# A four-layer graph network on one core: reordered ends, a tanh in two steps, and rows summed by accumulating DMA

## The chip, the core and the metric

The kernel runs on one core of a Trainium2 chip. The metric is the device time of one execution in microseconds. The engines named below are PE (TensorE: matmuls, with PEld for its weight loads), DVE (VectorE), ACT (ScalarE), POOL (GpSimd) and SP (SyncE, which here only issues DMA transfers).

## The reference, cut to what matters

64 graphs of 256 nodes with 128 features, all in fp32, go through four layers; every layer is a layernorm with ReLU ahead of it and a residual behind it. Layer 0 is the costly one: it needs a score for every pair of nodes, with a leaky ReLU over 256 features inside.

```python
# layer 0, W = adj
s1 = einsum('bkf,ef->bke', x, W[:, :F]);  s2 = einsum('bkf,ef->bke', x, W[:, F:])
pre = s1[:, :, None, :] + s2[:, None, :, :] + b_lin      # 256 x 256 pairs x 256 features
h = where(pre >= 0, pre, 0.2 * pre)
e = einsum('bije,e->bij', h, a) + bias
out = sigmoid(softmax(e, axis=2) @ x)
# layer 1
e = sigmoid(a_tgt + a_src + be) * mask;  recv = elu([e @ x_h, x_h * sum(e)] @ Wn + bn)
# layer 2: attention with A = exp(8 * tanh(q k / (8 sqrt(d)))) * adj
# layer 3: five steps of a gated update
for _ in range(5):
    m = adj @ h
    z = sigmoid([m, m] @ w3.T + h @ u3.T + b);  r = sigmoid([m, m] @ w4.T + h @ u3.T + b)
    hv = tanh([m, m] @ w5.T + (r * h) @ u5.T + b);  h = (1 - z) * h + z * hv
```

## The kernel before

**Groups.** The 64 graphs are cut into 34 groups (line 15): two of one graph, thirty of two, two of one. Layers 1 to 3 work on a group at a time; layer 0's pairs are made for one graph at a time.

**The pairs of layer 0** (class `Pairs`, from line 538). A graph has 32 rows of 8 receiving nodes each. For a row and each half `ec` of the 256 features there is a batch: one SBUF tile `r` of 128 partitions x 4 x 2 x 256 numbers, 8 KB in each partition and 1 MB in all, which holds max(s2, -s1) or relu(s2 + s1). A batch is made in two halves, and each half by whichever of three engines is free: DVE with one instruction (line 614), ACT with four (line 626), POOL with four (line 631). `r` has 11 buffers (`BUFS`). PE then reads a finished batch with eight matmul instructions (line 679) and adds it into the scores `e_ps`. So a row costs PE two batches. There is one way to save PE a batch: a *merged* row has only the batch of the first feature half made, and DVE adds the second half into it in place with eight instructions of line 648; then PE reads one batch. A row is merged when at least `SPARE` = 5 finished batches wait for PE as it begins.

**A planner writes the order of every engine's instructions.** The loop at the end of the function keeps a modelled time for PE, DVE, ACT and POOL (class `Model`) and, again and again, issues the step that can start first: a half, a merge, a batch for PE, or the next step of one of the chains. The chains are generators that give the name of the engine for the next step: `ahead` (layernorm and sender tiles of the next graphs), `behind` (layer 0's softmax), `chain12` (layers 1 and 2), `chain3` (layer 3, one group after another, and the constants at the start) and `chain4` (layer 3 of the last group alone). In the middle they are paced, so that chain work is spread. The order is fixed once it is written: on the chip each engine goes through its own list in order and waits for semaphores where the model was wrong.

**The start.** ACT issues the DMAs of the adjacency matrix, of layer 0's `a`, and of ten small vectors (all through line 139), and runs its first activation after them. `constants0` (line 216) sorts the features by the sign of `a` and makes `w_p` (the sorted, scaled weights, from four pairs of matmuls and one ACT copy, line 283), `blin_p`, `v2_rep` and what is needed for an odd feature. `head` (line 463) makes the first group's s1 and s1n, `senders` (line 512) its s2; pair making starts when s2 is there.

**The end.** After the last pair, the last group still goes through its softmax, layers 1, 2 and 3. `Home` (line 899) gives the last group's layer 3 banks and tiles of its own, so that it can run beside `chain3`. In a step of `layer3` (line 916) ACT runs the tanh of z and then the one of the candidate.

Of the kernel before, what the change touches and what calls it, by code (L numbers as in the profile page):

```python
# [8 lines left out]
F32 = mybir.dt.float32  # L9
AF = mybir.ActivationFunctionType  # L10
ALU = mybir.AluOpType
# [9 lines left out]
SPARE = 5  # L21
MARGIN = {"pe": 300}
MEMORY = 7000
# [13 lines left out]
class Model:  # L37
# [8 lines left out]
    def __init__(self):  # L46
        self.t = {"pe": 0.0, "dve": 0.0, "act": 0.0, "pool": 0.0}
# [6 lines left out]
def kernel(ctx: ExitStack, tc: tile.TileContext, ins: dict, out: bass.AP):  # L54
# [87 lines left out]
    def column(name):  # L142

        v = ins[name]
        return fetch(
            [P, v.shape[0] // P], "c_" + name, v.rearrange("(c p) -> p c", p=P), nc.scalar
        )

    order = ctx.enter_context(tc.manual_schedule())
    xts = [load_x(0)]  # L150
    adj_n = fetch([P, 2, N], "adj_n", adj.rearrange("(c p) m -> p c m", p=P), nc.scalar)
    a_col = column("L0_gnn_a")
    blin = column("L0_gnn_b_lin")
    ident = constant([P, P], "ident")
# [47 lines left out]
    bm_bc = fetch([P, P], "bm_bc", ins["L1_gnn_bm"].partition_broadcast(P), nc.scalar)  # L202
    be_bc = fetch([P, 1], "be_bc", ins["L1_gnn_be"].partition_broadcast(P), nc.scalar)
# [12 lines left out]
    def constants0():  # L216
# [10 lines left out]
        yield "dve"  # L227
        sgn, a_abs = col("sgn"), col("a_abs")
        dve(2).tensor_scalar(sgn, a_col, 0.0, None, ALU.is_ge)
        dve(2).scalar_tensor_tensor(a_abs, a_col, -1.0, a_col, ALU.mult, ALU.max)  # L230
        for c in range(2):
            dve(P).tensor_scalar(
                a_rep[:, c, :], a_rep[:, c, :], a_col[:, c : c + 1], None, ALU.mult
            )
# [7 lines left out]


        v2_ps = psum([P, P], "v2_ps")
        for c in range(2):
            mm(
                v2_ps, lhsT=adj_n[:, c, P : 2 * P], rhs=a_rep[:, c, :],
                start=(c == 0), stop=(c == 1),
            )
        yield "dve"  # L250
        bef = constant([P, 3], "bef")
# [22 lines left out]
        yield "pe"  # L274
        p = psum([P, 2, N], "w_p_ps")
        for half in range(2):
            for src in range(2):
                mm(
                    p[:, half, :], lhsT=adj_n[:, src, bass.ts(half, P)],
                    rhs=flat(perm[:, src, :, :]), start=(src == 0), stop=(src == 1),  # L280
                )
        yield "act"
        act(2 * N).copy(w_p, p)
        counts["w_p"] += 1
# [12 lines left out]
        p = psum([P, 4], "odd_ps")  # L297
        mm(p[:, 0:1], lhsT=ones, rhs=odd, start=True, stop=True)
        for c in range(2):
            for src in range(2):  # L300
                mm(
                    p[:, 1 + c : 2 + c], lhsT=perm[:, src, c, :], rhs=blin[:, src : src + 1],
                    start=(src == 0), stop=(src == 1),
                )
        yield "dve"
        dve(2).tensor_copy(blin_p, p[:, 1:3])
        dve(2).tensor_scalar(blin_n, p[:, 1:3], -1.0, None, ALU.mult)
        counts["w_p"] += 1
        odd_all = constant([P, 1], "odd_all")
        dve(1).tensor_copy(odd_all, p[:, 0:1])  # L310
# [104 lines left out]
    def ln_relu(space, xt, tag, ln, when=None):  # L415

        G = xt.shape[1]
        for g in range(G):
            if g % 2 == 0:
                yield "dve", when  # L420
            if g == 0:
                st = sp.tile([P, G, 6], F32, tag=tag + "_st", name="bst", bufs=2)
                mv = sp.tile([P, G, 2], F32, tag=tag + "_mv", name="bmv", bufs=2)
            dve(P).bn_stats(st[:, g, :], xt[:, g, :])
        yield "dve"
        for g in range(G):
            dve(6, more=15).bn_aggr(mv[:, g, :], st[:, g, :])  # L427
        yield "pool"

        ve = sp.tile([P, G], F32, tag=tag + "_ve", name="bve", bufs=2)  # L430
        minus = sp.tile([P, G], F32, tag=tag + "_mm", name="bmm", bufs=2)
        pool(277).tensor_scalar(ve, mv[:, :, 1], 1.0, LN_EPS, ALU.mult, ALU.add)  # L432
        pool(150).tensor_scalar(minus, mv[:, :, 0], -1.0, 0.0, ALU.mult, ALU.add)
        rstd = sp.tile([P, G], F32, tag=tag + "_rs", name="brs", bufs=2)
        pool(1085).tensor_tensor(rstd, ve, neg_half[:, 0:G], ALU.pow)
        shift = sp.tile([P, G], F32, tag=tag + "_sh", name="bsh", bufs=2)
        pool(302).tensor_tensor(shift, minus, rstd, ALU.mult)  # L437
        for g in range(G):
            if g % 2 == 0:
                yield "act"  # L440
            if g == 0:
                h = space.tile([P, G, P], F32, tag=ln, name=tag, bufs=3 if space is ap else 1)
            act(P, 2, 1).activation(  # L443
                h[:, g, :], xt[:, g, :], AF.Relu, bias=shift[:, g : g + 1],
                scale=rstd[:, g : g + 1],
            )
        return h
# [13 lines left out]


# [49 lines left out]
    def senders(b, of, to):  # L512

        h_t = flat(of["h_t"][:, 2 * b : 2 * b + 2, :])
        yield "pe"
        p = psum_h([P, 2, N], "s2_ps")
        for ec in range(2):
            mm(p[:, ec, :], lhsT=w_p[:, 1, bass.ts(ec, P)], rhs=h_t, start=True, stop=True)
        yield "act"
        s2 = ap.tile([P, 2, N], F32, tag="s2", name="s2")  # L520
        act(2 * N).copy(s2, p)
        to["s2"] = s2
        if "bound" not in of:
            yield from bounds(of)
        yield "pe"
        p = psum_h([P, N], "left_ps")
        mm(p, lhsT=left2, rhs=h_t, start=True, stop=True)
        for ic in range(2):
            yield "dve", None, of["bound_at"]
            if ic == 0:  # L530
                adj_l = ap.tile([P, 2, N], F32, tag="adj_l", name="adj_l", bufs=3)
            dve(N, 1).scalar_tensor_tensor(
                adj_l[:, ic, :], p, of["bound"][:, 2 * b + ic : 2 * b + ic + 1], adj_n[:, ic, :],
                ALU.min, ALU.add,
            )
        to["adj_l"] = adj_l

    class Pairs:
# [24 lines left out]
        def begin(self):  # L563
            waiting = sum(x["halves"] == 2 for x in self.batches)
            merged = waiting >= SPARE
            for ec in range(1 if merged else 2):
                batch = {"t": self.row, "ec": ec, "merged": merged, "halves": 0, "ready": 0.0}
                self.todo += [(batch, ec, 0), (batch, ec, 1)]
            self.row += 1
# [31 lines left out]
        def make(self, who):  # L601
# [33 lines left out]
            if batch["merged"]:  # L635
                self.merges.append((model.t[who] + LAG[who], batch, g2))
            else:
                self.whole(batch, who)

# [119 lines left out]
    def layer1(x1):  # L759
# [34 lines left out]
        for b in range(NB):  # L794
# [3 lines left out]
            yield "act"  # L798
            for jc in (1, 0):
                act(N, 1).activation(  # L800
# [98 lines left out]
    class Home:  # L899


        def __init__(self, aside):
            self.aside = aside

        def bank(self, shape, name, odd):
            if not self.aside:
                return psum(shape, name)
            space, tag = ((ps_d, "s2_dve"), (ps_c, "s2_act"))[odd % 2]
            return space.tile(shape, F32, tag=tag, name=name)

        def tile(self, W, tag, name, bufs=1):
            if not self.aside:
# [3 lines left out]
    def layer3(x3, hn, h_t, home):  # L916
        G, NB, W = sizes(x3)
        hf = flat(h_t)
        for step in range(STEPS):
            yield "pe"  # L920
            m_ps = home.bank([P, W], "m_ps", step)
# [6 lines left out]
            g_ps = home.bank([P, W], "gate_ps", step + 1)  # L928
# [5 lines left out]
            mm(g_ps, lhsT=ws["w4_w"], rhs=m_t, start=False, stop=True)  # L934
            yield "act"
# [6 lines left out]
            yield "pe"  # L942
            mm(
                g_ps, lhsT=w34_t, rhs=m_t, start=False, stop=True, skip_group_check=True
            )
            hv_ps = home.bank([P, W], "hv3_ps", step)
            mm(hv_ps, lhsT=ws["w5_w"], rhs=m_t, start=True, stop=False)
            mm(hv_ps, lhsT=u5_th, rhs=rh2, start=False, stop=True)
            yield "act"
            t_z, cand = g_ps, hv_ps  # L950
            act(W, 1).activation(t_z, g_ps, AF.Tanh, bias=bz, scale=0.5)  # L951
            yield "act"
            act(W, 1).activation(cand, hv_ps, AF.Tanh, bias=bh)  # L953
# [12 lines left out]
            if step < STEPS - 1:  # L966
                yield "pe"
                tp = home.bank([P, W], "hn_ps", step)
# [8 lines left out]
        tp = home.bank([P, W], "y_ps", step)  # L977
# [8 lines left out]
    def first_rest(g, x1):  # L986
# [5 lines left out]
        last = g == len(GROUPS) - 1  # L992
        (chain4 if last else chain3).add(last_rest(g, x3, hn, h_t, Home(last)))

    def last_rest(g, x3, hn, h_t, home):
        y = yield from layer3(x3, hn, h_t, home)
# [53 lines left out]
    chain4 = Chain(2400)  # L1050
    chains = [ahead, behind, chain3, chain12, chain4]
# [24 lines left out]
    ahead.add(head(xts[0], made[0]))  # L1076
# [3 lines left out]
    while True:  # L1080
        paced = n < len(graphs) - 2
        if not making and n < len(graphs) and "s2" in sent[n]:
            g, b = graphs[n]
            making.append(Pairs(g, b, made[g], sent[n]))
            multiplying.append(making[0])
# [3 lines left out]
        for e in ("pe", "dve", "act", "pool"):  # L1089
# [16 lines left out]
            if e == "dve":  # L1106
# [5 lines left out]
                if making and any(p is not making[0] and p.pending() for p in multiplying):  # L1112
                    continue
            if making and (freed or not making[0].fresh()):
# [6 lines left out]
        if step:  # L1121
            step(at, paced)
        elif what == "multiply":
# [3 lines left out]
            freed.append(model.t["pe"] + LAG["pe"])  # L1127
            if p.over:
# [51 lines left out]
```

## Time and profile before

| | before |
|---|---|
| median of the runs (lowest to highest) | 5137.93 us (5136.36 to 5138.56) |
| the profiled execution, device time | 5146.74 us |
| its span on the core | 5144.9 us |
| mean granted TensorE clock | 0.996 |
| matmuls of `e_ps` (line 679) | 27872, eight to a batch: 3484 batches |
| merging instructions (line 648) | 4896, eight to a merged row: 612 of 2048 rows |
| halves made by DVE / ACT / POOL | 1803 / 2615 / 2550 |

3484 batches and 612 merged rows are 4096, two for each row, and the three makers' halves sum to two for each batch. The busy shares of the page are a union of recorded spans. ACT's records overlap in the middle of the run (34 pair tiles recorded at 1.3 us each take 12.38 us from the first start to the last end), so the price of an ACT instruction there is read from a run of them and not from the mean of one. DMA-issuing instructions are not in the busy time.

### The profile page before, as it was taken

To read this page: it belongs to the slowest core of one execution; us is meant where nothing else is said; L and a number is where in the kernel's file an instruction comes from. 1 tells how busy PE (TensorE), PEld (TensorE's weight loads), DVE (VectorE), ACT (ScalarE), POOL (GpSimd) and SP (SyncE) were. 2 spreads that over 40 slices of the span, in tenths; PEclk is the share of its full clock that TensorE was granted. 3 is DMA by queue.
4 is the path that set the end of the run, shared out by engine and by line. 5 is a ranking of instruction groups with operands and counts; after the bars stand their busy time and mean duration, and the time that the engine had idled before them with its cause. 6 is when DMAs were issued, how large, how long until landed. Compare 5 with 4: busy or idle time off the path is not lost. (4 is left out here: it accounts for less than half of the span.)

```text
span 5144.9 us, 152945 instructions
## 1 busy us (share of the span) xinstructions
PE 5058.0 (98%) x57347; PEld 1988.1 (39%) x57347; DVE 4951.3 (96%) x9664; ACT 5034.1 (98%) x13196; POOL 4862.2 (95%) x10825
## 2 busy tenths in 40 slices
PE   8999999999999999999999999999999999999997
PEld 3334433334343343333344433333333334333343
DVE  7999999999999999999999999999999999999994
ACT  7999999999999999999999999999999999999994
POOL 8999999999999999999999999999999999999991
PEclk9999999999999999999999999999999999999999
DMA  0000000000000000000000000000000000000000
GB/s 20 6 2 5 5 6 6 4 4 6 6 6 6 2 6 6 6 6 2 6 6 6 6 2 6 6 6 6 2 6 6 6 6 5 2 5 4 4 6 6
DMA packets 56028, 28.10 MB, mean 5 GB/s; under 512 B 20337, under 2 KB 55281, under 8 KB 55281
## 3 DMA queue, kind: packets, MB, share of 16 engines
q1 hardware_dynamic: 53168, 17.97, 1.4%
q8 instruction: 449, 7.36, 0.6%
q14 instruction: 299, 2.44, 0.2%
q10 hardware_dynamic: 2112, 0.33, 0.0%
HBM read 9.84 MB, written 8.45 MB: 4 GB/s over the span
## 5 line engine op out<-in xcount | busy, mean ns | idle before, releaser
L631 POOL TENSOR_SCALAR r<-s,s1n 128x256 f32<-128x256 f32 x10200 | 4612.8, 475 | 81.0 <-PE e_ps L679 21.9
L626 ACT ACTIVATE r<-s_act,s 128x256 f32<-128x256 f32 x9948 | 4489.0, 1312 | 2.6 <-PE e_ps L679 2.6
L679 PE MATMUL e_ps<-r,a_win 128*32 128x512 f32 x27872 | 3330.9, 594 | 5.6 <-POOL r L631 2.3
L614 DVE TENSOR_TENSOR r<-s_dve,s1n 128x1024 f32<-128x1024 f32 x1803 | 2093.9, 1211 | 4.7
L648 DVE SCALAR_TENSOR_TENSOR r<-s_dve,s1n,r 128x256 f32<-128x256 f32 x4896 | 2002.3, 472 | 1.0 <-POOL r L631 1.0
L679 PEld LDWEIGHTS e_ps<-r,a_win 128*32 128x32 f32 x27872 | 958.1, 110 | 1734.4 <-issue 1255.6
L443 ACT ACTIVATE h<-x,bsh,brs 128x128 f32<-128x128 f32 x384 | 320.5, 1344 | 2.1 <-POOL bsh L437 2.1
L626 ACT ACTIVATE r<-s,s 128x256 f32<-128x256 f32 x512 | 311.1, 1207 | 0.0
L106 PE MATMUL m_ps<-adj_t,hn 128*32 128x256 f32 x4096 | 261.0, 388 | 3.1 <-ACT hn L974 3.0
L932 ACT COPY m_t<-m_ps 128x512 f32<-128x512 f32 (+1 forms) x170 | 229.4, 1349 | 15.8 <-PE m_ps L106 15.7
L951 ACT ACTIVATE gate_ps<-gate_ps,bz 128x512 f32<-128x512 f32 (+1 forms) x170 | 236.6, 1392 | 7.0 <-PE gate_ps L106 6.9
L953 ACT ACTIVATE hv_ps<-hv_ps,bh 128x512 f32<-128x512 f32 (+1 forms) x170 | 234.2, 1378 | 2.4 <-PE hv_ps L106 2.4
L938 ACT ACTIVATE m_ps<-gate_ps,br 128x512 f32<-128x512 f32 (+1 forms) x170 | 226.2, 1331 | 8.9 <-PE gate_ps L106 8.9
L974 ACT COPY hn<-hn_ps 128x512 f32<-128x512 f32 (+1 forms) x136 | 186.6, 1372 | 17.8 <-PE hn_ps L113 17.8
L106 PEld LDWEIGHTS m_ps<-adj_t,hn 128*32 128x32 f32 x4096 | 141.2, 112 | 132.0 <-issue 44.8
L106 PE MATMUL gate_ps<-m_t,t_w_w 128*32 128x512 f32 (+1 forms) x1360 | 173.3, 572 | 9.7 <-ACT m_t L932 9.0
L106 PE MATMUL gate_ps<-m_t,w_t 128*32 128x512 f32 (+1 forms) x1360 | 175.0, 569 | 5.0 <-ACT m_ps L938 5.0
L106 PE MATMUL hv_ps<-m_t,t_w_w 128*32 128x512 f32 (+1 forms) x1360 | 174.6, 567 | 0.0
L106 PE MATMUL hv_ps<-rh,u_th 128*32 128x512 f32 (+1 forms) x1360 | 174.5, 567 | 0.0
L432 POOL TENSOR_SCALAR bve<-bmv 128x4 f32<-128x4 f32 (+1 forms) x136 | 26.2, 193 | 128.7 <-DVE bmv L427 119.9
L106 PE MATMUL s_ps<-h0t,w_p 128*32 128x256 f32 (+1 forms) x1568 | 139.4, 449 | 5.4 <-ACT s1n L482 2.8
L106 PE MATMUL gate_ps<-hf,u_t 128*32 128x512 f32 (+1 forms) x1088 | 143.9, 574 | 0.0
(206 smaller groups left out, 5211.6 us busy)
## 6 DMA issues: line engine op xcount, KB each, us to landing
xt<-in_x_dram SPq DMA_DIRECT2D x30, 256.0 KB
out_dram<-y SPq DMA_DIRECT2D x30, 256.0 KB
row<-rows SPq DMA_DIRECT2D x128, 0.5 KB
xt<-in_x_dram SPq DMA_DIRECT2D x4, 128.0 KB
out_dram<-y SPq DMA_DIRECT2D x4, 128.0 KB
bound<-row SPq DMA_DIRECT2D x30, 2.0 KB
raw_L_gnn_w_w<-in_L_gnn_w_w_dram SPq DMA_DIRECT2D x3, 128.0 KB
adj_n<-in_adj_dram ACTq DMA_DIRECT2D x1, 256.0 KB
```

The costliest lines, as they stand in the source:

```text
L106: nc.tensor.matmul(out[bass.ts(c, 32), :], lhsT=lhsT[:, bass.ts(c, 32)], rhs=rhs, **flags)
L443: act(P, 2, 1).activation(h[:, g, :], xt[:, g, :], AF.Relu, bias=shift[:, g : g + 1], scale=rstd[:, g : g + 1],)
L614: nc.vector.tensor_tensor(r[:, 2 * g2 : 2 * g2 + 2, :, :], s2[:, ec : ec + 1, :].unsqueeze(1).to_broadcast([P, 2, 2, N]), self.s1n_v[:, ec ...
L626: nc.scalar.activation(r[:, g, ic, :], s2[:, ec, :], AF.Relu, bias=s1[:, ec, i : i + 1])
L631: nc.gpsimd.tensor_scalar(r[:, g, ic, :], s2[:, ec, :], FLT_MAX, s1n[:, ec, i : i + 1], ALU.min, ALU.max,)
L648: nc.vector.scalar_tensor_tensor(r[:, g, ic, :], self.own("dve")[:, 1, :], self.of["s1n"][:, 1, i : i + 1], r[:, g, ic, :], ALU.max, ALU.add,)
L679: nc.tensor.matmul(self.e_ps[bass.ts(g, 32), :, :].rearrange("p a b -> p (a b)"), lhsT=a_win[:, batch["ec"], 31 - t : 63 - t], rhs=flat(r[ ...
L932: act(W).copy(m_t, m_ps)
L938: act(W, 1).activation(t_r, g_ps, AF.Tanh, bias=br, scale=0.5)
L951: act(W, 1).activation(t_z, g_ps, AF.Tanh, bias=bz, scale=0.5)
L953: act(W, 1).activation(cand, hv_ps, AF.Tanh, bias=bh)
L974: act(W).copy(hn, tp)
```

## The change

Four things are done together.

1. **Rows summed by DMA.** When at least `QUEUE` = 5 finished batches wait for PE and POOL is between two halves, `send` takes the latest row whose two batches are both finished and unread, and POOL issues one accumulating DMA that adds the second batch's 1 MB into the first. The second buffer is given back when the transfer is modelled as landed; PE reads the first after that. The model takes 0.8 us of POOL for the issue, 5 us for a transfer (one at a time) and 2.5 us until it has landed. `SPARE` goes from 5 to 6.
2. **The start.** ACT's queue keeps two DMA issues, `a` ahead of the adjacency matrix; the small vectors go to SP. ACT runs a tanh on a dummy as its first activation. `constants0` makes `w_p` first, second half ahead of first and with a copy for each half, and `v2_rep` and the rest later. A new `first_head` makes the first group's s2, s1 and s1n in one go, with s1n on DVE. All four modelled times are set to at least ACT's when the first pairs begin, and nothing is paced until then.
3. **Layer 1's tanh** (two instructions on one bank) becomes two steps of the planner.
4. **The end.** The last two groups' layer 3 each get a chain and banks of their own (`chain5`: the two score banks and `ps_h`; `chain4`: `s2_dve` and `s2_act`), and both wait until all pairs have been made and read. For the last group the candidate's matmuls and tanh come ahead of z's.

```diff
-SPARE = 5
+QUEUE = 5
+ISSUE, TRANSFER, LANDED = 800, 5000, 2500
+SPARE = 6
+LANDS = 3400
...
+        def pair(self):
+            waiting = [x for x in self.batches if x["halves"] == 2]
+            now = model.t["pool"] + 100
+            if sum(x["ready"] <= now for x in waiting) < QUEUE:
+                return None
+            rows = [
+                x["row"] for x in waiting
+                if not x["merged"] and x["ec"] == 0 and len(x["row"]) == 2 and x["row"][1] in waiting
+                and max(y["ready"] for y in x["row"]) <= now
+            ]
+            return max(rows, key=lambda r: max(r[0]["ready"], r[1]["ready"])) if rows else None
+
+        def send(self):
+            low, high = self.pair()
+            self.batches.remove(high)
+            model.op("pool", ISSUE)
+            nc.gpsimd.dma_start(
+                out=low["r"].rearrange("p a b n -> p (a b n)"),
+                in_=high["r"].rearrange("p a b n -> p (a b n)"), accum_op=ALU.add,
+            )
+            model.dma = max(model.dma, model.t["pool"]) + TRANSFER
+            low["ready"] = model.dma + LANDED
+            low["merged"] = True
+            freed.append(low["ready"])
+            freed.sort()
...
+            if e == "pool" and model.dma <= model.t[e] + 0:
+                for p in multiplying:
+                    if p.pair() and (best is None or model.t[e] <= best[0]):
+                        best = (model.t[e], "send", p)
...
 # start
-    adj_n = fetch([P, 2, N], "adj_n", adj.rearrange("(c p) m -> p c m", p=P), nc.scalar)
-    a_col = column("L0_gnn_a")
+    a_col = column("L0_gnn_a", nc.scalar)
+    adj_n = fetch([P, 2, N], "adj_n", adj.rearrange("(c p) m -> p c m", p=P), nc.scalar)
     blin = column("L0_gnn_b_lin")
+    table = constant([P, 1], "table")
+    nc.vector.memset(table, 0.0)
+    nc.scalar.activation(table, table, AF.Tanh)
...
-    ahead.add(head(xts[0], made[0]))
+    ahead.add(first_head(xts[0], made[0], sent[0]))
...
-        paced = n < len(graphs) - 2
+        paced = 0 < n < len(graphs) - 2
...
+            if n == 0:
+                model.t = {e: max(t, model.t["act"]) for e, t in model.t.items()}
...
+    def first_head(xt, to, snd):
...
+        h = yield from ln_relu(ap, xt, "h0", "h0", at=LANDS)
+        h_t = yield from transpose_blocks(ap, h, "h0t", psum_h)
...
+        yield "pe", lambda: counts["w_p"] > 1
+        s2_ps, s1_ps = psum_h([P, 2, N], "s2_ps"), psum_a([P, 2, W], "s1_ps")
+        for half, p in ((1, s2_ps), (0, s1_ps)):
+            for ec in range(2):
+                mm(
+                    p[:, ec, :], lhsT=w_p[:, half, bass.ts(ec, P)], rhs=flat(h_t),
+                    start=True, stop=True,
+                )
+        yield "dve"
...
 # layer 1
-            yield "act"
             for jc in (1, 0):
+                yield "act"
...
 # end
+        LAST = ((ps_e, "e"), (ps_e, "e"), (ps_h, "ps_h"))
+        LAST_BUT_ONE = ((ps_d, "s2_dve"), (ps_c, "s2_act"))
...
+            early = home.banks is home.LAST
+            if early:
+                hv_ps = home.bank([P, W], "hv3_ps")
+                mm(hv_ps, lhsT=ws["w5_w"], rhs=m_t, start=True, stop=False)
...
+        lane = {len(GROUPS) - 1: chain5, len(GROUPS) - 2: chain4}.get(g, chain3)
+        lane.add(last_rest(g, x3, hn, h_t, Home(g)))
...
+        if home.banks:
+            yield "pe", lambda: n == len(graphs) and not (making or doing or multiplying)
```

## The prediction

> **What bounds the kernel now.** I read the page's busy shares and slices first, then the groups by cost, then a table of stretches, and last the timelines of both ends.
>
> ```profile
> PE 5058.0 (98%) x57347; PEld 1988.1 (39%) x57347; DVE 4951.3 (96%) x9664; ACT 5034.1 (98%) x13196; POOL 4862.2 (95%) x10825
> ```
> ```profile
> L631 POOL TENSOR_SCALAR r<-s,s1n 128x256 f32<-128x256 f32 x10200 | 4612.8, 475 | 81.0 <-PE e_ps L679 21.9
> L626 ACT ACTIVATE r<-s_act,s 128x256 f32<-128x256 f32 x9948 | 4489.0, 1312 | 2.6 <-PE e_ps L679 2.6
> L679 PE MATMUL e_ps<-r,a_win 128*32 128x512 f32 x27872 | 3330.9, 594 | 5.6 <-POOL r L631 2.3
> L614 DVE TENSOR_TENSOR r<-s_dve,s1n 128x1024 f32<-128x1024 f32 x1803 | 2093.9, 1211 | 4.7
> L648 DVE SCALAR_TENSOR_TENSOR r<-s_dve,s1n,r 128x256 f32<-128x256 f32 x4896 | 2002.3, 472 | 1.0 <-POOL r L631 1.0
> ```
>
> Four engines are full at once, and none has a releaser of any size in front of its main group. So no single wait bounds the middle: its length is where the four loads meet, and what moves it is work taken off all of them together. Note the L648 row: DVE gives 2 ms to merging, only to spare PE batches.
>
> ```profile
> 24.00:40.00 16.00, 16.00 (x94) 3.32 (x86) 8.88 (x11) 10.92 (x30) 16.00 (x36) 1.00 0.02 3
> 40.00:60.00 20.00, 17.71 (x131) 5.10 (x131) 16.82 (x37) 10.31 (x30) 19.65 (x44) 1.00 0.00 1
> ```
> ```profile
> 2000.00:3000.00 1000.00, 993.46 (x11316) 396.72 (x11312) 982.10 (x1899) 999.60 (x2616) 969.93 (x2157) 1.00 0.02 5
> ```
> ```profile
> 5043.00:5097.00 54.00, 40.72 (x496) 17.71 (x492) 18.97 (x47) 20.65 (x46) 4.44 (x14) 0.87 0.02 6
> 5097.00:5143.00 46.00, 33.94 (x498) 15.54 (x490) 15.86 (x38) 17.32 (x43) 0.00 (x0) 0.96 0.02 5
> ```
>
> Columns are length, then PE, PEld, DVE, ACT, POOL, clock, DMA share, GB/s. The middle thousand is full, POOL least (30 us idle); the DMA engines stand at 2%. The ends are not full: the first pairs start late, and from 24 to 60 us DVE idles 10.3 us and ACT 14.8 us while POOL runs without a gap:
>
> ```profile
> 23.92 29.63 POOL L631 TENSOR_SCALAR r<-s,s1n 128x256 f32<-128x256 f32 x64 [16.41 <-ACT s L521]
> ```
>
> The last 100 us, after the last pair is read at 5043, are one latency chain.
>
> **What the Trainium skill says.** (1) "DMA: Bandwidth & Descriptors", section "Latency and other measured facts", puts the first byte of a DMA issued from GpSimd at about 1 us, by the descriptors that POOL's own cores write. No DMA of this kernel is issued from POOL; its SP and ACT issues show 0.33 to 0.49 us each. (2) The same page, "Anatomy of one DMA", gives 2.0 us + bytes / 436 GB/s: 1 MB is an estimated 4.4 us. (3) "Collectives: The Full Stack", section on the bandwidth ceiling, says an add in the DMA engines needs two source reads and so runs at half a copy's rate: estimate 2 x 2.4 = 4.8 us of engine time and 2 us of landing. No run here shows either; the plan's 5 + 2.5 us agree. (4) "TensorE: Matmul & The Clock Gate", Part 1: after some 3.4 us idle PE runs at half its clock. The trace agrees in kind: in the last step, alone, the `m_ps` matmuls take 1.81 us, against 1.07 beside another chain.
>
> **1. Rows by DMA.** Unit costs, from runs of one kind in the timelines: a batch on PE 0.86 us (24 of its instructions in 2.58), a DVE half 1.14 (seven in 8.00), a merge instruction 0.40 (13 in 5.15), an ACT tile 0.36 (34 in 12.38), a POOL tile 0.452 (40 in 18.10). From 2000 to 3000 there are 5600 matmuls, so 700 batches, 960 merges, so 120 merged rows, together 820/2 = 410 rows; halves 366 (DVE), 520 (ACT), 510 (POOL). What remains of 1000 us is each engine's chain work and slack:
>
> - PE 1000 - 700 x 0.86 = 398
> - DVE 1000 - 366 x 1.14 - 960 x 0.40 = 199
> - ACT 1000 - 520 x 1.44 = 251
> - POOL 1000 - 510 x 1.81 = 77, of which 30 idle
>
> Now let those 410 rows take T, with d rows summed by DMA, none merged, and POOL's issue at c. PE needs 0.86 x (820 - d) + 398 = T; the makers need (T - 199)/1.14 + (T - 251)/1.44 + (T - 77 - c d)/1.81 = 1640 halves, 120 x 2 more than now. For c = 0.8: at T = 985, d = 137, and the halves are 689 + 509 + 441 = 1639. So T falls by 15 in 1000: about 75 us over the roughly 5000 us of the middle. One DMA each 985/137 = 7.2 us fits a plan of one per 5 us, though POOL sends only between halves of 1.81 us and five batches must wait, so some merging will remain. With d = 100 and 40 merged rows (40 x 3.2 = 128 us of DVE; 1560 halves) the same sums meet near T = 991, a gain of 45. I take 50, between the two, nearer the mixed case.
>
> The issue's cost c is the unknown. Below stands the SP/ACT issue, 0.49; above, the skill's 1 us, with descriptor writing possibly held up longer. I take 0.8, between them. The order is fixed by a plan that believes 0.8, so each 0.1 us more is 690 x 0.1 = 69 us on POOL (690 = 137 x 5.0), of which its 30 us per 1000, 150 in all, are cover. Behind the issue stand POOL's next tiles, and PE waits for those. Below 0.8 nothing is gained past POOL's own idle time, since the plan doesn't know. The transfer itself is beside the engines; PE finds its row last among five waiting ones, so that some 3 x 0.86 us of other batches cover a late landing. The two buffers are held 8.3 us, 137 x 2 x 8.3 = 2270 of 11 x 985 = 10835 buffer-us: a fifth, and makers hardly wait for buffers now (21.9 and 2.6 us in the rows above). `SPARE` 6 only shifts rows from merging to sending. Queues: SP gets nothing of this.
>
> **2. The start.** ACT's first activation comes at 11.79, behind twelve DMA issues and a 1.28 us table load from 10.49, though its input `bsh` is done at 7.5. Now two issues end near 1.7, the load and the dummy near 3.3, so h starts near 7 (xt still lands at 3.9; layernorm on DVE and POOL takes to 7.5 now, less the constants that stood in between), h and its transposes and copy end near 9. `a` lands no later than 5.2; the chain from `sgn` to `perm` took 5.24 to 9.11 with 0.6 of a_abs and a_rep, now later: perm near 8.5. Then w_p's matmuls, 3.64 at PE's cold rate: 12.2; copy of the second half hidden, of the first 0.4; s2 1.3 and s1 1.3 on PE: 15.0; s1n 0.7 on DVE: 15.7. Pairs began at 23.9: 8 us gained. What moved back (v2_rep, `left`, adj_t: 3 us of PE, 2 of DVE) still has to be done, inside the full stretch: 1 us of the common length. SP's ten extra issues (0.4 each) delay the third x load by 4 us, to 17, and the weights, first needed beyond 47 us: nothing.
>
> From 24 to 60 PE takes its batches tile by tile from POOL (PEld waits 18.6 us for L631), because the model thought POOL free since the start and gave it 64 tiles in a row. Levelling the times mends that: 10.3 + 14.8 us idle and some 15 us of PE at a quarter of its packing, over four engines, is 10 us; I take 7. Start: 8 - 1 + 7 = 14, bounds 7 and 18.
>
> **3. Layer 1's tanh.** The same two instructions, with pair tiles allowed between: nothing, either sign under 1 us.
>
> **4. The end.** Before, group 33's steps run in lockstep with group 32's at 9.2 us (5106.41 to 5115.61), because 32 stands behind 31 in `chain3` until 5084. Now 32 can start at 5043, and most of it ends before 33 starts at 5097. A step alone, by its gaps and with the candidate first (0.43 saved before u5's matmul, 0.5 behind z's tanh), comes to 6.75 us warm; the cold PE adds some 1.4, as the last step shows: 8.1. Five steps gain 5.5. Against that, 32's 5 x 3.5 us of matmuls land between 5043 and 5097, where PE had 13 idle: 33's layers 1 and 2 are later by an estimated 0 to 5. I take +4, bounds -3 and +11.
>
> **Sum.** 50 + 14 + 4 = 68: span 5144.9 - 68 = 5077. The profiled execution was 1.8 above its span and 8.8 above the median, so 5146.7 - 68 - 8.8 = 5070 for the median.
>
> **Rivals.** *A, few sends, or the gain eaten.* If c is near 1.05, or five waiting batches are rare, the middle comes out as before; only the ends remain: 5138 - 18 = 5120. For it: the sums meet on a flat optimum. Against: 120 merges per 1000 us show that five batches waited that often. *B, POOL becomes the bound (slower).* POOL has 50 us of the forecast and 150 of idle time to give; it decides from c = 0.8 + 200/690 = 1.09 us. At 1.3: 345 us more on POOL, less 150, less 50, less the ends' 18: 5138 + 127 = 5265. For it: the skill's 1 us is close. Against: its other issue rows are a third to a half of that. *C, transfers slower than one per 7.2 us* queue up, and PE stands before rows that have not landed: at 8 us, 690 x 8 = 5520. For it: two reads and a write of 1 MB; against: idle DMA engines.
>
> **How the numbers follow.** Forecast 0.62, its own range 5030 (75 in the middle, 18 + 11 at the ends, and some of POOL's idle time used) to 5100; A 0.20, B 0.14, C 0.04. 0.2% is 10 us, what a measurement of this kernel can tell from no change. Faster: 0.62 and three quarters of A, 0.77; within: the rest of A, 0.05; slower: B and C, 0.18. The range, 5028 to 5125, reaches over A's time and leaves out B, C and little else.
>
> **What would show it.** POOL's DMA issues counted near 500 to 700, with 0.8 us between the tiles beside them; L648 down from 4896 to under 1700, L679 down to about 27200, L614 up by half; POOL's idle share down. First pairs near 16 us, no 64 POOL tiles in a row. Steps of the last group under 8.5 us. I am wrong if POOL tiles stand behind issues longer than 1.1 us, if PEld waits for DMA on `r`, or if L648 hardly falls.

## The result and the profile after

The changed kernel takes 5205.5 us (median of four runs, 5203.54 to 5205.89) where the kernel before takes 5137.17 us beside it: a ratio of 1.0133 [1.0118, 1.0148]. It is slower by 1.3%, 68 us, where 68 us of gain were forecast. The profiled execution has a span of 5203.6 us at a mean clock of 0.997.

First the groups of the page after. Columns are line, engine, operation, output from input, shape and count, then busy us and mean ns of one, then the idle time just before them and what ended most of it. Lines 675, 670, 751, 658 and 720 are the former 631, 626, 679, 614 and 648.

```profile
PE 5061.1 (97%) x57235; PEld 1963.0 (38%) x57235; DVE 4928.5 (95%) x8440; ACT 5000.4 (96%) x13112; POOL 4797.3 (92%) x10541
...
L675 POOL TENSOR_SCALAR r<-s,s1n 128x256 f32<-128x256 f32 x9672 | 4392.9, 510 | 172.6 <-DMA r<-r 141.2
L670 ACT ACTIVATE r<-s_act,s 128x256 f32<-128x256 f32 x9864 | 4342.3, 1006 | 110.5 <-DMA r<-r 108.5
L751 PE MATMUL e_ps<-r,a_win 128*32 128x512 f32 x27760 | 3314.0, 594 | 30.5 <-DMA r<-r 12.0
L658 DVE TENSOR_TENSOR r<-s_dve,s1n 128x1024 f32<-128x1024 f32 x2416 | 2809.4, 1211 | 52.4 <-DMA r<-r 44.1
...
L720 DVE SCALAR_TENSOR_TENSOR r<-s_dve,s1n,r 128x256 f32<-128x256 f32 x3056 | 1256.9, 472 | 2.8 <-POOL r L675 1.7
...
L702 POOL DMA_DIRECT2D r<-r x244 | 194.6, 798 | 68.0 <-ACT r L670 23.3
...
r<-r POOLq DMA_DIRECT2D x244, 1024.0 KB, 7.4
```

Three things are to be seen. The work moved as meant, if by less: DVE has 1840 merging instructions fewer and makes 613 halves more, PE has 112 matmuls fewer. But idle time grew, and on the *makers*: all three now stand before `r`, released by `DMA r<-r`, where before only POOL had idle time of any size (81.0 us), and PE's reading ended the largest part of it (21.9 us). And there are 244 sends, not 690; 382 rows (3056 / 8) are still merged. The table of waits says who pays for the DMAs (us in total, times, longest):

```profile
POOL r L675 <- DMA r<-r: 141.2, 73, 6.0
...
ACT r L670 <- DMA r<-r: 109.4, 68, 5.6
...
DVE r L658 <- DMA r<-r: 44.1, 31, 4.2
...
PEld e_ps L751 <- DMA r<-r: 19.7, 14, 3.9
```

That is 141.2 + 109.4 + 44.1 = 295 us in 172 waits on the three makers, and 20 us on PE's weight loads, where the forecast looked for trouble. A maker reads nothing that a DMA writes. It can only stand there because the buffer it is to *write* is still the source of a transfer. The timeline shows it once (start, length, engine, instructions in a run, and in brackets the idle time before the run):

```profile
4988.59 0.80 POOL L702 DMA_DIRECT2D r<-r  x1
...
4989.31 3.69 POOL L675 TENSOR_SCALAR r<-s,s1n 128x256 f32<-128x256 f32 x8
...
4996.20 1.83 POOL L675 TENSOR_SCALAR r<-s,s1n 128x256 f32<-128x256 f32 x4 [3.21 <-DMA r<-r]
4996.24 3.49 DVE L658 TENSOR_TENSOR r<-s_dve,s1n 128x1024 f32<-128x1024 f32 x3 [3.26 <-DMA r<-r]
```

POOL goes on 0.72 us after it began the issue, makes two more halves, and then stops together with DVE at about 4993.0: both want the two halves of one new batch, and the buffer it was given is the one that POOL's DMA is reading. It lands 7.5 us after the issue, and both go on.

The middle thousand in the table of stretches (columns as in the prediction):

```profile
2000.00:3000.00 1000.00, 985.10 (x11021) 376.68 (x11024) 958.80 (x1632) 976.42 (x2554) 943.92 (x2069) 1.00 0.31 63
```

Every engine is emptier than before, by 8 (PE) to 26 us (POOL). Counted as rows that PE reads, 402.0 are done in 1000 us (mean of 1000 to 4000), against 407.8 before.

The start, in the timeline and the stretches:

```profile
15.52 1.84 POOL L675 TENSOR_SCALAR r<-s,s1n 128x256 f32<-128x256 f32 x4 [10.26 <-DVE s1n L489]
```
```profile
20.00:40.00 20.00, 19.66 (x212) 8.50 (x209) 19.89 (x27) 19.59 (x55) 20.00 (x46) 1.00 0.02 3
40.00:60.00 20.00, 19.90 (x174) 6.70 (x166) 19.93 (x30) 19.43 (x55) 18.34 (x41) 1.00 0.01 1
```

Pairs begin at 15.52 us, and from 20 to 60 us PE, DVE, ACT and POOL hardly idle (most on POOL, 1.7 us). By 300 us 128.5 rows are done, against 122.0 before.

The end, in PE's timeline; each line is the `m_ps` product that opens a step of layer 3, with `h` in a group's first step and `hn` in its others, x32 for a group of two graphs and x16 for one of one. First the line before of group 31, the last of two graphs, then the lines after:

```profile
5003.27 1.91 PE L106 MATMUL m_ps<-adj_t,h 128*32 128x256 f32 x32
```
```profile
5083.33 1.91 PE L110 MATMUL m_ps<-adj_t,h 128*32 128x256 f32 x32
...
5105.00 1.05 PE L110 MATMUL m_ps<-adj_t,h 128*32 128x256 f32 x16
...
5163.81 1.04 PE L110 MATMUL m_ps<-adj_t,h 128*32 128x256 f32 x16
5172.29 1.07 PE L110 MATMUL m_ps<-adj_t,hn 128*32 128x256 f32 x16 [0.46 <-ACT hn L1061]
5179.19 1.07 PE L110 MATMUL m_ps<-adj_t,hn 128*32 128x256 f32 x16 [0.46 <-ACT hn L1061]
...
5186.10 1.07 PE L110 MATMUL m_ps<-adj_t,hn 128*32 128x256 f32 x16 [0.46 <-ACT hn L1061]
5193.00 1.07 PE L110 MATMUL m_ps<-adj_t,hn 128*32 128x256 f32 x16 [0.46 <-ACT hn L1061]
```

The last group's first step takes 8.5 us, and its others 6.9, where before they were 9.2 apart. But group 31 has its *first* step at 5083.33, 11 us before the last pair is read (5094.7); before, it had run it 40 us ahead of that point (5003.27 of 5043.4). So three groups share the end instead of two. The last group starts layer 3 at 5163.81, 69 us after the pairs' end, against 54 before, and the end is 108.9 us long, not 101.5.

### The profile page after: what moved, and what is told of

Its sections match the earlier page's. It is cut to its first block, busy times and chain, and to the rows that moved or that the text cites. A ratio compares the mean times of both kernels' runs of the same rounds, so it can differ in the third digit from the quotient of the medians.

```text
span 5203.6 us, 151033 instructions
## 1 busy us (share of the span) xinstructions
PE 5061.1 (97%) x57235; PEld 1963.0 (38%) x57235; DVE 4928.5 (95%) x8440; ACT 5000.4 (96%) x13112; POOL 4797.3 (92%) x10541
## 3 DMA queue, kind: packets, MB, share of 16 engines
q0 software_dynamic: 35136, 255.87, 24.4%
## 5 line engine op out<-in xcount | busy, mean ns | idle before, releaser
L675 POOL TENSOR_SCALAR r<-s,s1n 128x256 f32<-128x256 f32 x9672 | 4392.9, 510 | 172.6 <-DMA r<-r 141.2
L670 ACT ACTIVATE r<-s_act,s 128x256 f32<-128x256 f32 x9864 | 4342.3, 1006 | 110.5 <-DMA r<-r 108.5
L658 DVE TENSOR_TENSOR r<-s_dve,s1n 128x1024 f32<-128x1024 f32 x2416 | 2809.4, 1211 | 52.4 <-DMA r<-r 44.1
L720 DVE SCALAR_TENSOR_TENSOR r<-s_dve,s1n,r 128x256 f32<-128x256 f32 x3056 | 1256.9, 472 | 2.8 <-POOL r L675 1.7
L702 POOL DMA_DIRECT2D r<-r x244 | 194.6, 798 | 68.0 <-ACT r L670 23.3
L452 ACT ACTIVATE h<-x,bsh,brs 128x128 f32<-128x128 f32 x384 | 235.8, 900 | 6.1 <-POOL bsh L446 3.7
L1038 ACT ACTIVATE gate_ps<-gate_ps,bz 128x512 f32<-128x512 f32 (+1 forms) x170 | 192.7, 1133 | 7.1 <-PE gate_ps L110 6.9
L1010 ACT COPY m_t<-m_ps 128x512 f32<-128x512 f32 (+1 forms) x170 | 185.4, 1090 | 10.8 <-PE m_ps L110 10.6
L1061 ACT COPY hn<-hn_ps 128x512 f32<-128x512 f32 (+1 forms) x136 | 139.4, 1025 | 13.1 <-PE hn_ps L117 12.9
L872 ACT ACTIVATE th_ps<-th_ps,a_src 128x256 f32<-128x256 f32 x128 | 143.3, 1120 | 1.3 <-PE th_ps L110 1.3
```

Source lines behind the costliest of these rows:

```text
L452: act(P, 2, 1).activation(h[:, g, :], xt[:, g, :], AF.Relu, bias=shift[:, g : g + 1], scale=rstd[:, g : g + 1],)
L658: nc.vector.tensor_tensor(r[:, 2 * g2 : 2 * g2 + 2, :, :], s2[:, ec : ec + 1, :].unsqueeze(1).to_broadcast([P, 2, 2, N]), self.s1n_v[:, ec ...
L670: nc.scalar.activation(r[:, g, ic, :], s2[:, ec, :], AF.Relu, bias=s1[:, ec, i : i + 1])
L675: nc.gpsimd.tensor_scalar(r[:, g, ic, :], s2[:, ec, :], FLT_MAX, s1n[:, ec, i : i + 1], ALU.min, ALU.max,)
L702: nc.gpsimd.dma_start(out=low["r"].rearrange("p a b n -> p (a b n)"), in_=high["r"].rearrange("p a b n -> p (a b n)"), accum_op=ALU.add,)
L720: nc.vector.scalar_tensor_tensor(r[:, g, ic, :], self.own("dve")[:, 1, :], self.of["s1n"][:, 1, i : i + 1], r[:, g, ic, :], ALU.max, ALU.add,)
```

## The experiments

Twelve kernels were run, each timed against the kernel before on the same chip. There were several chips, on which the kernel before takes 5136 to 5146 us, so runs are compared by their ratios. "Pairs' end" is when PE has read the last pair in the profiled execution, "end" what remains of the span.

| run | edit | device us | ratio [95%] | pairs' end | end | sends / merged rows |
|---|---|---|---|---|---|---|
| after | - | 5205.5 | 1.0133 [1.0118, 1.0148] | 5094.7 | 108.9 | 244 / 382 |
| e1_no_sends | no sends, `SPARE` 5 | 5109.05 | 0.9930 [0.9914, 0.9947] | 5010.7 | 93.8 | 0 / 601 |
| e2_no_sends_spare6 | no sends, `SPARE` 6 | 5100.42 | 0.9913 [0.9898, 0.9928] | 5004.8 | 95.6 | 0 / 557 |
| e3_own_slots | the buffer the plan means | 5096.33 | 0.9904 [0.9889, 0.9919] | 4982.0 | 113.1 | 244 / 382 |
| e4_quarter | DMAs of a quarter | 5094.28 | 0.9901 [0.9887, 0.9916] | 4980.5 | 113.4 | 244 / 382 |
| e5_tanh | before, tanh split alone | 5125.65 | 0.9978 [0.9969, 0.9987] | 5021.7 | 102.5 | 0 / 612 |
| e6_fifo_known | the plan knows the buffers' order | 5224.97 | 1.0171 [1.0155, 1.0186] | 5133.4 | 89.5 | 228 / 277 |
| e7_own_q3_s8 | own slots, `QUEUE` 3, `SPARE` 8 | 5108.4 | 0.9945 [0.9931, 0.9960] | 4989.5 | 116.4 | 570 / 99 |
| e8_own_pace | own slots, pace 2200 | 5068.64 | 0.9867 [0.9852, 0.9882] | 4977.5 | 89.6 | 250 / 379 |
| e9_no_sends_pace | no sends, `SPARE` 6, pace 2200 | 5083.66 | 0.9897 [0.9882, 0.9912] | 4992.4 | 91.7 | 0 / 561 |
| e10_after_pace | pace 2200 | 5161.79 | 1.0050 [1.0035, 1.0065] | 5072.5 | 88.7 | 250 / 379 |
| e11_own_q4_pace | own slots, `QUEUE` 4, pace 2200 | 5066.78 | 0.9866 [0.9851, 0.9880] | 4975.6 | 88.8 | 372 / 288 |
| e12_own_pace2000 | own slots, pace 2000 | 5056.19 | 0.9841 [0.9825, 0.9858] | 4965.5 | 91.8 | 252 / 357 |

### Without sends

The expectations speak of two theories. By the *slot theory* what costs is which buffer a new batch is given (the next section); by the *theory of held buffers* it is that a transfer keeps two of eleven away, whichever they are.

```diff
-QUEUE = 5
+QUEUE = 99
...
-SPARE = 6
+SPARE = 5
```

> The changed kernel without its DMA sums and with SPARE back at 5, so both ends and the tanh alone. All theories: the middle runs as before (410 rows in the thousand us from 2000), merged rows again near 600, no wait of a maker for a DMA. The start gives 8 to 15 us, the end takes up to 8: 5120 to 5140, against 5137 before and 5205 changed. If it stays above 5180, the loss is not in the DMA sums at all.

> As the one before, but with SPARE at 6: only the merging threshold is moved. If the raised threshold costs by itself (more finished batches waiting, buffers short), this is slower than the run with 5 by some tens of us and its makers wait for PE; the slot theory and the theory of held buffers both expect within 15 us of the run with 5, 5115 to 5150.

 (the same edit with `SPARE` left at 6)

The loss goes with the sends: without them the change is faster than before by 0.7%, and by 0.9% with `SPARE` 6. So the other three parts gain, and part 1 costs over 100 us (2.0 and 2.2% of 5137). Both times lie below their expected ranges: the other parts bring more than was thought (36 us in the first run, with an end of 93.8 us against 101.5).

### Which buffer a new batch gets

All batches of the changed kernel share one tag, `r`, with eleven buffers. The planner keeps a sorted list of the times at which buffers come free, and believes that a new batch gets the earliest. The program's allocator decides otherwise: counted over the instructions of the two programs, a new batch takes the buffer whose last reader was *issued* earliest, in 3498 of 3498 cases before, and in 3193 of 3753 after (the second earliest in the other 560). A DMA counts as a reader when it is issued, not when it lands. While PE was the only last reader the two orders were the same. With sends, the source buffer of a DMA was handed out again after a median of 5 to 6 further batches (2 to 10). 3714 batches (4096 less the 382 merged) in some 5080 us of pair making are one per 1.37 us, so that is 7 to 8 us later, often less, and the DMA takes 7.4. The first experiment gives every buffer a tag of its own and has the planner name the one that it means (the last two groups' layer 3 tiles, which shared the tag, get fixed buffers); with it such a buffer comes back after a median of 9 batches.

```diff
-                batch["r"] = rp.tile([P, 4, 2, N], F32, tag="r", name="r")
+                batch["slot"] = self.slot
+                batch["r"] = rp.tile(
+                    [P, 4, 2, N], F32, tag="r%d" % self.slot, name="r", bufs=1
+                )
...
-            freed.append(low["ready"])
+            freed.append((low["ready"], high["slot"]))
...
-    freed = [0.0] * BUFS
+    freed = [(0.0, k) for k in range(BUFS)]
...
-                freed.pop(0)
+                p.slot = freed.pop(0)[1]
```

The second leaves the buffers alone and makes the transfer short instead; three quarters of each sum are left out:

```diff
-                out=low["r"].rearrange("p a b n -> p (a b n)"),
-                in_=high["r"].rearrange("p a b n -> p (a b n)"), accum_op=ALU.add,
+                out=low["r"].rearrange("p a b n -> p (a b n)")[:, 0:512],
+                in_=high["r"].rearrange("p a b n -> p (a b n)")[:, 0:512], accum_op=ALU.add,
```

> The changed kernel with the buffer of each r tile picked by the planner: the one that its model has free first, instead of the one whose last reader was issued first. Eleven buffers, sends and their size stay. Slot theory: the buffer of a row in transit is now taken again after more batches, makers' waits for the DMA on r fall from 295 us in all to under 90, time 5060 to 5120. Theory of held buffers (two of eleven away for 8 us leave too few, whichever is taken): waits stay near 295 or turn into waits for PE, time 5180 to 5210.

> The changed kernel with every instruction in its place, but each DMA adds only the first 512 of the 2048 numbers of a partition, so that the sums of rows are left incomplete in three quarters. Slot theory: it lands after 4 to 5 us instead of 7.4, the buffer is back when its next user comes, waits for the DMA fall from 295 us to under 100, time 5090 to 5150. Theory that the planned order itself is short of buffers, or that POOL's issue is what costs: nothing changes, 5190 to 5210, since the issue and the order are the same.

The same groups in the page with own slots (lines 678, 673, 661 stand for 675, 670, 658):

```profile
L673 ACT ACTIVATE r<-s_act,s 128x256 f32<-128x256 f32 x9864 | 4557.0, 1418 | 1.2 <-PE e_ps L755 1.2
L678 POOL TENSOR_SCALAR r<-s,s1n 128x256 f32<-128x256 f32 x9672 | 4401.1, 537 | 38.7 <-PE e_ps L755 12.5
...
L661 DVE TENSOR_TENSOR r<-s_dve,s1n 128x1024 f32<-128x1024 f32 x2416 | 2808.1, 1211 | 6.3 <-PE e_ps L755 0.2
...
r<-r POOLq DMA_DIRECT2D x244, 1024.0 KB, 7.4
```

And in the page with a quarter of each transfer:

```profile
L675 POOL TENSOR_SCALAR r<-s,s1n 128x256 f32<-128x256 f32 x9672 | 4401.0, 522 | 60.6 <-DMA r<-r 17.4
...
r<-r POOLq DMA_DIRECT2D x244, 256.0 KB, 3.3
```

Own slots keep every instruction count, every send and the 7.4 us of landing, and the makers' 295 us of waiting are gone, with 2.3% of the time (ratio 1.0133 to 0.9904, some 118 us). A transfer that lands in 3.3 us, with the buffers handed out as in the change, does the same: 0.9901, with some 20 us of such waits left. What the two share is that a buffer is no longer wanted before its transfer has landed, and that is the cause; POOL's issues, the queue of DMAs and the traffic itself are the same in e3 as after, and cost little. The 295 us are waits of three engines, partly at once, so that they are worth less in time than their sum.

### Would it do if the plan knew the order?

A rival was that the allocator is harmless and the harm is the planner's ignorance of it. Here the list is no longer sorted, so it is close to the order in which buffers are really handed out, and the plan sees the wait coming.

```diff
             freed.append(low["ready"])
-            freed.sort()
...
             freed.append(model.t["pe"] + LAG["pe"])
-            freed.sort()
```

> The changed kernel with the planner's list of free buffers no longer sorted, so that it hands them out in the order in which their last readers were issued, as the program does, and knows when a maker will have to wait. Slot theory: the surprise is gone, waits for the DMA on r fall from 295 us to under 120, but the plan itself has makers held back: 5110 to 5160, between the kernel with slots of its own (5096) and the changed one. Theory that only the longer hold counts and not who gets the buffer: it stays near 5200.

```profile
POOL r L675 <- DMA r<-r: 130.5, 77, 4.6
...
ACT r L670 <- DMA r<-r: 91.8, 59, 5.0
...
DVE r L658 <- DMA r<-r: 64.0, 40, 5.0
```

The forecast of this run was missed. The waits are as large as in the change (286 us), only foreseen: the planner itself reckons 293 us of makers waiting for buffers, where in the change it reckons 14. The time is 1.7% over the kernel before. With makers held back, fewer rows are merged, 277 and not 382, so PE reads 121 batches more (27760 matmuls to 28728), some 104 us at 0.86 each. This planner, at least, doesn't get around a bad order by knowing it; giving out another buffer does.

### The tanh alone

```diff
-            yield "act"
             for jc in (1, 0):
+                yield "act"
```

> The kernel before with layer 1's tanh in two steps and nothing else. The prediction gave it nothing (within 10 us of before). Rival: the run with both ends but without sends was faster in the middle too (409.8 rows in a thousand us from 1000 to 4000, against 407.8), and this is the only part of it that acts there; then this gains 12 to 22 us.

A ratio of 0.9978 [0.9969, 0.9987], 11 us. The prediction had put nothing here. What it frees is not shown by a single row: the waits of this run differ from those before by a few us each. The pace of the middle is 409.3 rows per 1000 us, 0.4% above 407.8. That a different order of everything after it does it can't be excluded.

### More sends

```diff
-QUEUE = 5
+QUEUE = 3
...
-SPARE = 6
+SPARE = 8
```

(on top of own slots)

> Buffers picked by the planner, and sends from three finished batches on (QUEUE 3), merges from eight (SPARE 8): 570 sends and 99 merged rows, where the changed kernel has 244 and 382. The balance of loads gives 988 us for 410 rows, against 996 for the counts of the changed kernel: 35 to 40 us less than the run with own slots, 5050 to 5070. Rival: eleven buffers are too few for twice the rows in transit; then makers wait for PE or the DMA by 100 us and more in all, and it is no faster than 5096.

This brings the sends near the number that the prediction assumed, 570 in all and 123 per 1000 us of the middle, with 99 merged rows left. The forecast was missed and its rival came: the run is slower than with 244 sends, 0.9945 against 0.9904. From 1000 to 4000 us the pace is 412.8 rows per 1000 us, against 411.9, so the balance of loads that was to give 8 in 1000 (996 to 988) gives 2; and from 4000 to 4960 us PE reads 380.6 rows, where it reads 385.5 with 244 sends. Waits and one stretch of this run:

```profile
POOL r L678 <- PE e_ps L755: 52.8, 45, 4.8
...
PEld e_ps L755 <- DMA r<-r: 45.3, 46, 3.2
...
DVE r L661 <- PE e_ps L755: 33.7, 35, 2.3
...
PE e_ps L755 <- DMA r<-r: 29.6, 19, 4.7
```
```profile
2000.00:3000.00 1000.00, 980.82 (x11120) 377.37 (x11116) 977.40 (x1369) 993.38 (x2603) 957.16 (x2044) 0.99 0.66 133
```

Makers stand before buffers that PE has not read (53 + 34 + 16 us with ACT's), and PE before sums that have not landed (75 us); another 41 us are makers' waits for transfers. The likely reading is that eleven buffers are too few to have several waiting for PE and two in each transfer; a run with more of them was not made. Two sizes were changed at once here, so their shares are not told apart.

### The end, and what the sends are worth

`chain3` is paced: a figure says how far apart in modelled time its steps may be issued. It was left at 2400 while the pairs got quicker in the plan: by the planner's own clock they end at 4891 us, 40 us sooner than before (4931), and what remains takes 119 us and not 102. So the plan itself has the longer end.

```diff
-    ahead, behind, chain3, chain12 = Chain(1500), Chain(2500), Chain(2400), Chain(2200)
+    ahead, behind, chain3, chain12 = Chain(1500), Chain(2500), Chain(2200), Chain(2200)
```

> Buffers picked by the planner, and chain3 paced at 2200 instead of 2400. With own slots the pairs ended 29 us sooner than without sends (4982 against 5011), but the tail behind them took 113 us instead of 94. If layer 3's chain had fallen behind by its pace, the tail shrinks by 10 to 20 us: 5076 to 5088. If the lag has another cause, within 5 us of 5096.

> The changed kernel without sends (SPARE 6) and with chain3 paced at 2200. It tells what the sends are worth once buffers and tail are in order. If they are worth the 23 us by which the pairs ended sooner with own slots (4982 against 5005 without sends), this stands 15 to 30 us above the run with own slots and the same pace (5069): 5085 to 5100. If the sends are worth next to nothing and the pace did it, 5065 to 5080.

> The changed kernel as it is, buffers in the order of issue, with chain3 paced at 2200. Slot theory: the middle's loss stays (makers' waits for the DMA near 290 us) and only the tail shrinks by 10 to 20 us: 5180 to 5200. If the pace of chain3 is what made the changed kernel slow, it falls to 5110 or below.

PE's timeline with own slots and the new pace:

```profile
4911.41 1.91 PE L110 MATMUL m_ps<-adj_t,h 128*32 128x256 f32 x32
...
4977.35 1.05 PE L110 MATMUL m_ps<-adj_t,h 128*32 128x256 f32 x16
...
5026.44 1.07 PE L110 MATMUL m_ps<-adj_t,h 128*32 128x256 f32 x16
```

Group 31 is back ahead of the pairs' end (4977.5), by 66 us; group 32 starts as the pairs end, as part 4 meant it to; the last group follows 49 us after it and not 69. The end takes 89.6 us, against 113.1 with own slots at the old pace; the time falls by more than was expected. So the longer end after the change is the pace's doing and no fault of the new chains. Run e10, the change with this figure alone, fell further than expected: 20 us at the end, and the pairs end 22 us sooner too, with the makers' waits for DMAs down from 295 to 217 us (102.0 on POOL, 75.5 on ACT, 39.2 on DVE).

With the end set right in both, e8 less e9 is what the sends themselves bring: 5083.66 - 5068.64 = 15 us. On the two pairs of ratios it is 0.3%, and their intervals touch at 0.9882.

### On from there

> Own slots and pace 2200, with sends from four finished batches on: 372 sends and 288 merged rows, against 250 and 379. By the balance of loads 10 to 15 us less than 5069; by the run with 570 sends, where makers began to wait for buffers (some 100 us for PE, 40 for the DMA), no gain: 5065 to 5080.

> Own slots with chain3 paced at 2000. The tail behind the last pair was 113 us at 2400 and 90 at 2200. If the lag of layer 3's chain is gone at 2200, no more than 5 us are left: 5062 to 5072; if it still runs behind, 5045 to 5060.

`QUEUE` 4 makes 372 sends in place of 250 and gives no difference (0.9866 and 0.9867). A pace of 2000 gives 5056.19 us, 0.9841 [0.9825, 0.9858], the best of all: 1.6% under the kernel before. The time lies in the range that was expected if layer 3 still ran behind, but not for that reason: the end is no shorter (91.8 us). The 12 us come before the pairs' end. They are in the plan (by the planner's clock the pairs end at 4885 us and not 4898); what in the plan makes them was not looked into.

## Why the prediction was wrong

**The step that failed** is in "1. Rows by DMA": "The two buffers are held 8.3 us, 137 x 2 x 8.3 = 2270 of 11 x 985 = 10835 buffer-us: a fifth, and makers hardly wait for buffers now". It asked *how many* buffers are left over and never *which one* a maker gets next. By the same sum the 244 sends that came held 244 x 2 x 8.3 = 4050 of 11 x 5080 = 55880 buffer-us, 7%, and the makers still waited. In the code before, one tag with eleven buffers turns over in the order of issue, and that was harmless as long as PE's reads ended in that order. A DMA that is issued early and ends late breaks it, and a maker then stands before one held buffer while others are free. This is 295 us of waits where none was, and some 118 us of time (94 with `chain3` paced at 2200 in both). None of the rivals had it: B looked for POOL's issue, C for the DMA engines, A for too few sends, which came too, but A reckoned with no loss from them. Of the three signs named for being wrong, none decides: POOL's issues stay at 0.80 us, PE's waits for DMAs came but are 32 us in all, the merges are down by 38%. The idle column of the makers' rows was the place to look.

**The size of the gain in the middle** was wrong as well, and by itself would have left a smaller win. Taken at 50 us, it is 15 in e8 against e9. Part of it is the number: 244 sends, not 690, since the plan seldom has five batches waiting with two of one row, a free POOL and a free transfer (with four it sends 372). But the number is not all. In e7, with 570, the makers and PE waited for each other through the eleven buffers, and the balance of loads, which knows no buffers, promised more than came. Here too the sum over buffer-us looks like the weak term: it counted the buffers under transfer, and not those that must lie ready besides. And the forecast's own sum for its mixed case, redone, is T = 992 for the makers and not 991, so that its 45 us are nearer 40: a trifle.

**What was right in it.** The issue: 0.80 us recorded (798 ns mean), 0.72 us from its start to POOL's next tile above, against 0.8 taken. That it fits is in part luck: 0.8 was taken between the issue of another engine and a time to a first byte, and neither is the price of such an issue. POOL did not become the bound, so B falls. The landing: 7.4 us against the plan's 7.5. The queue's share of the engines, 24.4% of the span in the page, is 0.244 x 5203.6 / 244 = 5.2 us for each, well under C's 7.2. The estimate from the Trainium skill ("Collectives: The Full Stack", the bandwidth ceiling, for an add at half a copy's rate, and "DMA: Bandwidth & Descriptors", "Anatomy of one DMA", for the fixed part) was 4.8 + 2 = 6.8 us. The quarter transfers allow that to be taken apart, as an estimate from two sizes: 7.4 for 1 MB and 3.3 for a quarter give 4.1 us for 0.786 million bytes, 192 GB/s, and 1.9 us that don't depend on size. The fixed part agrees with the page's 2.0 us, and the rate lies somewhat below half of its 436 GB/s.

**The start** was right: 14 us forecast with pairs from 15.7 us; they begin at 15.52, and the 6.5 rows gained by 300 us are worth 6.5 / 0.408 = 16 us.

**Layer 1's tanh** was put at nothing, under 1 us either way; alone it is 11 us. The forecast put the term at nothing without a sum; how the gain arises is not shown.

**The end** was forecast 4 us shorter and came out 7 us longer. The cost of a step alone was right, 6.75 us warm and 8.1 cold: here most take 6.9 us, with `m_ps` runs of 1.07 us, but with own slots they take 7.7 to 8.6 us, with runs of up to 1.93, so that the short steps of this run are luck. But the step of the argument "Now 32 can start at 5043, and most of it ends before 33 starts" took it for granted that group 31 is done by then. `chain3` ran on its old pace while the pairs became quicker in the plan, and group 31 had only begun by then (5083.33 of 5094.7); with a pace of 2200 alone the end is 88.7 us.

In sum, against the kernel before: the start some 15 us faster, the tanh 11, the sends 15, the end 7 slower, and buffers that come back too early 118 at the old pace or 94 at the new one. That makes 60 to 84 us slower, where 68 were measured; the parts do not simply add.

## What to carry to other kernels

When a buffer of a rotating set gets a reader that ends late, ask which buffer is handed out next, not how many are free: an allocator that goes by the order of issue can return the late one first, and giving each buffer a name of its own lets the plan choose. In the profile this shows as a maker that waits for a transfer whose data it never reads. And when one part of a hand-paced schedule is made quicker, the paces of the others have to be set again before its worth can be read.

## What had not been expected of the hardware

The landing of an accumulating transfer of 1 MB within SBUF hardly depended on how many there were: 7.4 us with 244 in the run, 7.6 with 570, where the DMA engines were busy 66% of the middle. Its issue took POOL longer when there were more, 0.93 us with 570 against 0.80 with 244.
